# Left-operand loads on another queue, scores between projection products, values behind them, and a pinned order on TensorE and SyncE

## The chip, the core and the metric

The kernel runs on one core of a Trainium2 chip. A core has five engines, each with its own instruction stream: TensorE (PE; its weight loads are listed as PEld), VectorE (DVE), ScalarE (ACT), GpSimd (POOL) and SyncE (SP). SP computes nothing; it only issues transfers (DMAs). ACT and POOL issue transfers too, in line with their own work. What is measured is the time of one execution on the device, in microseconds (us). The median of three runs of the kernel before is 3149.64 us (3143.34 to 3151.75); its profiled execution took 3153.26 us.

## The reference

A transformer block on x of 4 sequences (b), 512 positions, width 1024, all in float32. xn is the layer norm of x. One branch is attention with 32 query heads in 8 groups (g) of 4, one key and one value head per group, head width 128, RMS norm on queries and keys, a linear position bias with a causal mask. The other is a gate: a linear layer with a mixture of low-rank updates, then SiLU.

```
q, k, v = xn @ Wq.T, xn @ Wk.T, xn @ Wv.T          # split into heads
q, k    = rmsnorm(q, q_norm_w), rmsnorm(k, k_norm_w)
scores  = q k^T / sqrt(128) + slope * (pos_k - pos_q), masked above the diagonal
s       = (softmax(scores) @ v) @ Wo.T
base    = xn @ W.T + bias + sum_n (2 * lora_weights[n]) * (xn @ A[n].T) @ B[n].T
out     = x + s * silu(base)
```

## The kernel before

**Three stages.** The first stage normalises and transposes x, keeps the operands of the projections in DRAM (`xs`), and computes the first half of the gate. The second stage, which the change touches, runs over 32 *units*, a unit being a pair (g, b), g outermost, and then computes the second half of the gate for the four sequences (`last_gate`). The third stage multiplies by Wo and combines the branches.

**Projection of a unit.** `project` (L205) computes q, k and v of a unit with Strassen's scheme in one level: for each of two row halves m there are 7 products instead of 8, each of 4 matmuls of 128x128 by 128x384. A unit thus has 14 products, numbered 1 to 14 here. `strassen` (L121) is a generator that stops after each product, so that a caller can put other work between them. Every product takes its own left operand `a`, 256 KB, which `stream` (L396) fetches from `xs` at L399. The pool has 6 buffers for `a`, so the load for a product has to wait until the product six before it is done. Partial sums go through ACT copies (`save`, L215) and DVE additions (`put`, L222 and L224). After 7 products `norm` (L410) takes two of the four row tiles: ACT squares them (L414), DVE sums (L416, L418), POOL takes the inverse root (L420), DVE scales (L421) and transposes in 32x32 blocks into `flat` (L424). After product 14 the other two tiles follow, and then 16 small transfers on SP move the blocks of `flat` into `qkT` (L433); DVE scales the keys into `kT` (L438).

**Scores of a unit.** `attend` (L449) makes 16 score tiles, c = 0 to 15, of 128 rows by 32(c+1) columns (at least 128). For each: a PE matmul into one of 3 PSUM buffers `sc` (L456), on DVE the bias and a row minimum (L465), on ACT the exponential with its row sum into `pr` (L476), which frees the `sc` buffer. Once four tiles are through, DVE takes the reciprocal of the sums (L490), ACT scales the four (L495), and DVE transposes them blockwise into `turned` (L497), of which there is one buffer. When all 16 are done, 16 transfers on SP, of 160 KB each, move `turned` into `pt` (L505), one buffer again.

**Values of a unit.** `values` (L511) makes four tiles `ov` with 1, 2, 3 and 4 matmuls (128x128 by 128x512) from `pt` and v (L516). ACT copies each out (`oh`, L524, two buffers) and issues its store `ot` (L525).

**The loop** (L579 to L590). For a unit, `fill` is the generator of the next unit's projection. The values of the unit before are written with one step of `fill` after each of their four tiles, then the scores with one step after every two tiles, then the rest of `fill`.

**What sets the order.** The program is recorded and then ordered by a planner with its own estimate of durations. It may move an instruction past others of its engine wherever data allow; the text above is only its input. Each engine then executes its own list strictly in that order, and an instruction that waits holds all that stand behind it. Buffers that are still read or written, and data not yet there, become waits on semaphores. Transfers that SP and ACT issue share eight completion counters, dealt out in turn in the planner's order; before a transfer is issued, it waits until the one eight places before it has landed, whichever of the two queues issued that one.

In the order that the planner made of the kernel before, PE has in each unit: products 1 to 4 of the next projection, the ten matmuls of the values of the unit before, score tiles 0 and 1, then products with two score tiles between them up to product 11, then products 12 to 14 (half of product 10 stands before and half behind score tile 11). SP has per unit 16 `pt` transfers, 16 `qkT` transfers, then 14 `a` loads.

Of the kernel before, what the change touches and what calls it, by code (L numbers as in the profile page):

```python
# [37 lines left out]
NP = 7  # L38


def _slopes():
    start = 2 ** (-(2 ** (-(math.log2(H) - 3))))
    return [start * start**i for i in range(H)]
# [3 lines left out]
def kernel(  # L47
# [14 lines left out]
):  # L62
    nc = tc.nc
    slopes = _slopes()

    const = ctx.enter_context(tc.tile_pool(name="const", bufs=1))
    dram = ctx.enter_context(tc.tile_pool(name="dram", bufs=1, space=DRAM))
# [53 lines left out]
    def strassen(psum, snap, name, nk, ncols, lhs, rhs, shape, save, put):  # L121

        def product(acc, i, start):
            left, right = lhs(i), rhs(i)
            for k in range(nk):
                nc.tensor.matmul(  # L128
                    acc,
                    lhsT=left[k],  # L130
                    rhs=right[k],
                    start=start and k == 0,
                    stop=k == nk - 1,
                    skip_group_check=True,
                )

        def bank(n):
            return psum.tile([P, ncols], F32, tag="mm", name=f"{n}_{name}")

        def kept(n):  # L140
            return snap.tile(shape, F32, tag="kept", name=f"{n}_{name}")

        u = bank("u")
        product(u, A11B11, True)
        k1 = kept("k1")
        save(k1, u, 11)
        yield
# [37 lines left out]
    with ExitStack() as front:  # L185
# [70 lines left out]
        with ExitStack() as early:  # L256
# [19 lines left out]
            for n in range(NLORA):  # L276
                nc.scalar.dma_start(
                    out=coef[n * RANK : (n + 1) * RANK, :],
# [18 lines left out]
            def add_lora(half):  # L297
                for kc in range(KC):
                    pl = ps_sc.tile([P, 512], F32, tag="sc", name=f"pl_{half}_{kc}")
                    nc.tensor.matmul(  # L300
                        pl,
                        lhsT=laT[:, kc, :],
                        rhs=lb_sb[:, half * 512 : (half + 1) * 512],
                        start=True,
                        stop=True,
                    )
                    w = wfs[half][:, kc].rearrange("p n h -> p (n h)")
                    nc.vector.tensor_tensor(w, w, pl, ALU.add)
# [49 lines left out]
            for b in range(B):  # L358
# [11 lines left out]
                for n, _ in enumerate(work):  # L370
                    if b + 1 < B and n in (2, 9):
                        m = n // 7
# [8 lines left out]
        with ExitStack() as mid:  # L381
# [14 lines left out]
            def stream(name, b):  # L396
                def left(m, i):
                    a = apool.tile([P, KH, P], F32, tag="a", name=f"a_{name}_{m}_{i}")
                    nc.sync.dma_start(out=a, in_=xs[b][m][:, i])  # L399
                    return a  # L400

                return left


            def project_qkv(u, b, right, held):
                flat = unit.tile([P, NT, 4, G + 1, 32], F32, tag="flat", name=f"flat_{u}", bufs=1)
                v = unit.tile([P, NT, HD], F32, tag="v", name=f"v_{u}", bufs=3)
                held["v"] = v

                def norm(t, c):  # L410
                    nc.gpsimd.tensor_copy(v[:, t, :], c[:, G + 1, :])  # L411
                    qk = c[:, 0 : G + 1, :]
                    sq = work.tile([P, G + 1, HD], F32, tag="sq", name=f"sq_{u}_{t}", bufs=1)
                    nc.scalar.activation(sq, qk, AF.Square)  # L414
                    ss = small.tile([P, G + 1], F32, tag="ss", name=f"ss_{u}_{t}")
                    nc.vector.tensor_reduce(ss, sq, AX.X, ALU.add)  # L416
                    ms = small.tile([P, G + 1], F32, tag="ms", name=f"ms_{u}_{t}")
                    nc.vector.tensor_scalar(ms, ss, 1.0 / HD, RMS_EPS, ALU.mult, ALU.add)  # L418
                    inv = small.tile([P, G + 1], F32, tag="inv", name=f"inv_{u}_{t}")
                    nc.gpsimd.tensor_tensor(inv, ms, neg_half, ALU.pow)  # L420
                    nc.vector.tensor_tensor(  # L421
                        qk, qk, inv.unsqueeze(2).to_broadcast([P, G + 1, HD]), ALU.mult
                    )
                    nc.vector.transpose(  # L424
                        flat[:, t], qk.rearrange("p h (a e) -> p a h e", a=4)
                    )

                yield from project(f"p_{u}", b, G + 2, stream(u, b), right, norm)

                qkT = unit.tile([P, NT, 4, G + 1, 32], F32, tag="qkT", name=f"qkT_{u}", bufs=1)  # L430
                for a in range(4):
                    for r in range(4):
                        nc.sync.dma_start(  # L433
                            out=qkT[32 * a : 32 * a + 32, :, r].rearrange("p t h e -> p t (h e)"),
                            in_=flat[32 * r : 32 * r + 32, :, a].rearrange("p t h e -> p t (h e)"),
                        )
                kT = unit.tile([P, 4 * NT, 32], F32, tag="kT", name=f"kT_{u}", bufs=1)
                nc.vector.tensor_scalar(  # L438
                    kT,
                    qkT.rearrange("p t r h e -> p (t r) h e")[:, :, G, :],  # L440
                    w_sb,
                    None,
                    ALU.mult,
                )
                held.update(qkT=qkT, kT=kT)
                yield


            def attend(u, g, b, held, bias):  # L449
                qkT, kT = held["qkT"], held["kT"].rearrange("p c e -> p (c e)")  # L450

                def scores(i, t, den):
                    c = 4 * i + t
                    w = max(32 * (c + 1), P)
                    sc = ps_sc.tile([P, S], F32, tag="sc", name=f"sc_{u}_{c}")
                    nc.tensor.matmul(  # L456
                        sc[:, :w],
                        lhsT=qkT[:, i, t, 0:G, :].rearrange("p h e -> p (h e)"),
                        rhs=kT[:, :w],
# [22 lines left out]
                for i in range(NT):  # L482
# [8 lines left out]
                    for t in range(NT):  # L491
                        c = 4 * i + t
                        n = max(c + 1, 4)
                        pr = prs[t][:, : 32 * n]
                        nc.scalar.activation(pr, pr, AF.Copy, scale=rden[:, t : t + 1])  # L495
                        c0 = 4 * first_pair[i]
                        nc.vector.transpose(  # L497
                            turned[:, c0 : c0 + n, t, :],
                            pr.rearrange("p (n e) -> p n e", n=n),
                        )  # L500
                pt = unit.tile([P, npairs, G, P], F32, tag="pt", name=f"pt_{u}", bufs=1)
                src = turned.rearrange("p (n m) t e -> p n m (t e)", m=4)
                for h in range(G):
                    for m in range(4):
                        nc.sync.dma_start(  # L505
                            out=pt[32 * m : 32 * m + 32, :, h, :],
                            in_=src[32 * h : 32 * h + 32, :, m, :],
                        )
                held["pt"] = pt

            def values(u, g, b, held):  # L511
                pt, v = held["pt"], held["v"]
                for i in range(NT):
                    ov = ps_ov.tile([P, S], F32, tag="ov", name=f"ov_{u}_{i}")
                    for j in range(i + 1):
                        nc.tensor.matmul(  # L516
                            ov,
                            lhsT=v[:, j, :],
                            rhs=pt[:, first_pair[i] + j].rearrange("p h q -> p (h q)"),
# [12 lines left out]

            def load_qkv(g):
                raw[g] = weight_tile(G + 2, f"w_{g}")
                nc.sync.dma_start(
                    out=raw[g][:, :, 0:G, :],
                    in_=wq[g].rearrange("p k (n h) -> p k n h", n=G),
                )
                nc.sync.dma_start(
                    out=raw[g][:, :, G:, :],  # L540
                    in_=wkv[g].rearrange("p k (n h) -> p k n h", n=2),
                )
# [25 lines left out]
            def bias_of(g):  # L568
# [3 lines left out]
                )  # L572
                return bias

            load_qkv(0)
            for _ in start_project(*units[0]):
                pass
            before = None
            for n, (g, b) in enumerate(units):  # L579
                if b == 0:  # L580
                    bias = bias_of(g)
                fill = start_project(*units[n + 1]) if n + 1 < len(units) else last_gate(0)
                if before is not None:
                    for _ in values(f"{before[0]}_{before[1]}", *before, held.pop(before)):
                        next(fill, None)
                for _ in attend(f"{g}_{b}", g, b, held[g, b], bias):
                    next(fill, None)
                for _ in fill:
                    pass
                before = g, b  # L590
            fill = last_gate(1)
            for _ in values(f"{before[0]}_{before[1]}", *before, held.pop(before)):
                next(fill, None)
            for _ in fill:
                pass
            for b in range(2, B):
                for _ in last_gate(b):
                    pass


    with ExitStack() as back:
        wpool = back.enter_context(tc.tile_pool(name="wo", bufs=4))
        apool = back.enter_context(tc.tile_pool(name="heads", bufs=2))
# [166 lines left out]
```

## Time and profile before

| | us |
|---|---|
| median of the runs shown (lowest, highest) | 3149.64 (3143.34, 3151.75) |
| the profiled execution, and its span | 3153.26, 3151.5 |
| first scores (start of the units' steady run) | at 240.83 |
| start of the values in the first and in the thirtieth unit | at 279.25 and 2125.33 |
| end of the second stage on PE, start of the third | at 2323.0 and 2337.7 |
| PE busy, of the span | 2826.4 (90%) |
| DVE, ACT, POOL busy | 1315.5, 838.2, 562.3 |

The values start 29 times between 279.25 and 2125.33, so that a unit takes 63.66 us on average (1846.08 / 29). In the profile an arrow names what a wait ended on; a transfer is written destination<-source, SPq and ACTq are the issuing queues, and buffer numbers are left out of names, so that `u_p` and `c_p` are PSUM tiles of a projection.

### The profile page before, as it was taken

The numbers are of one execution on the slowest core, as the hardware profiler recorded it, in microseconds if no ns is written. First come the engines' busy times: TensorE is split into PE (matmuls) and PEld (weight loads), VectorE is DVE, ScalarE is ACT, GpSimd is POOL, SyncE is SP. The second block draws the span as 40 slices with busy tenths as digits, with TensorE's granted clock in tenths as the row PEclk, the third lists the DMA queues.
The fourth block names the chain that finished last, engine by engine and source line by source line (L and its number), as shares of the span: only waits on it lengthen the run. The fifth ranks groups of instructions, "written<-read, shape, count | busy, mean of one in ns | idle before, by whom it ended". The sixth has DMA issues, their size and how long they took to land.

```text
span 3151.5 us, 26438 instructions
## 1 busy us (share of the span) xinstructions
PE 2826.4 (90%) x8104; PEld 1551.5 (49%) x8104; DVE 1315.5 (42%) x3003; ACT 838.2 (27%) x2132; POOL 562.3 (18%) x532
## 2 busy tenths in 40 slices
PE   6898998989898989898989888988889999999997
PEld 4765554545454545454545444544654444344443
DVE  4225443454345434444445445443332232323464
ACT  1113433343343333333334333433200000000010
POOL 5430120121020120121012102011030031311311
PEclk9999999999999989999999999998989999999999
DMA  7544465555555556446546555465662333434364
GB/s 270 221 128 133 120 180 146 143 160 137 143 168 143 138 142 185 120 126 187 157 120 168 142 156 152 122 147 145 211 232 108 113 138 122 173 127 140 134 218 148
DMA packets 392220, 485.73 MB, mean 154 GB/s; under 512 B 31760, under 2 KB 269328, under 8 KB 389520
## 3 DMA queue, kind: packets, MB, share of 16 engines
q1 hardware_dynamic: 360032, 391.75, 44.8%
q10 hardware_dynamic: 20272, 50.34, 4.3%
q0 software_dynamic: 11776, 41.95, 3.3%
q8 instruction: 66, 1.08, 0.1%
q14 instruction: 74, 0.61, 0.1%
HBM read 265.82 MB, written 92.27 MB: 114 GB/s over the span
## 4 chain that ended last, share of the span: by engine, by line
PE 52%; SPq 16%; DVE 13%; POOL 7%; DMA 6%; issue 3%; ACT 3%; ACTq 0%; POOLq 0%; DVEq 0%
PE c_o L128 13%; SPq L505 11%; PE u_o L128 10%; PE c_p L128 9%; PE sc L456 6%; PE ov L516 6%; SPq L433 5%; PE u_p L128 5%; DVE turned L497 3%; POOL inv L420 3%; PE c_f L128 2%; DMA qkT<-flat 2%; DVE c_p L421 2%; PE u_f L128 2%; DVE flat L424 2%
## 5 line engine op out<-in xcount | busy, mean ns | idle before, releaser
L516 PE MATMUL ov<-pt,v 128*128 128x512 f32 x640 | 356.3, 722 | 151.7 <-DMA qkT<-flat 116.1
L456 PE MATMUL sc<-kT,qkT 128*128 128x128 f32 (+12 forms) x1024 | 311.8, 424 | 78.8 <-ACT pr L476 63.8
L128 PE MATMUL u_p<-t_q,a 128*128 128x384 f32 x1024 | 377.1, 508 | 2.5 <-DMA a<-xs 2.2
L128 PE MATMUL c_p<-t_q,a 128*128 128x384 f32 x1024 | 352.0, 487 | 2.0 <-DMA a<-xs 1.7
L128 PE MATMUL c_p<-w,a 128*128 128x384 f32 x1024 | 352.9, 487 | 0.0
L476 ACT ACTIVATE pr<-sc,low 128x128 f32<-128x128 f32 (+12 forms) x512 | 251.5, 493 | 341.2 <-DVE low L465 333.1
L516 PEld LDWEIGHTS ov<-pt,v 128*128 128x128 f32 x640 | 147.1, 236 | 353.6 <-issue 329.6
L465 DVE CUSTOM_DVE_ANT_0 sc<-sc,bias 128x128 f32<-128x128 f32 (+12 forms) x512 | 225.6, 459 | 212.9 <-PE sc L456 208.7
L456 PEld LDWEIGHTS sc<-kT,qkT 128*128 128x128 f32 x1024 | 186.2, 199 | 213.9 <-ACT pr L476 91.2
L411 POOL COPY v<-c_p 128x128 f32<-128x128 f32 x128 | 37.1, 294 | 1357.8 <-DVE c_p L222 1218.7
L128 PEld LDWEIGHTS u_p<-t_q,a 128*128 128x128 f32 x1024 | 199.2, 197 | 144.4 <-issue 29.9
L128 PEld LDWEIGHTS c_p<-t_q,a 128*128 128x128 f32 x1024 | 192.1, 190 | 134.5 <-issue 12.0
L128 PEld LDWEIGHTS c_p<-w,a 128*128 128x128 f32 x1024 | 194.2, 191 | 123.8
L128 PE MATMUL u_o<-t_o,s 128*128 128x512 f32 x512 | 236.3, 605 | 17.5 <-DVE k_o L676 17.3
L495 ACT ACTIVATE pr<-pr,rden 128x128 f32<-128x128 f32 (+12 forms) x512 | 236.5, 522 | 15.9 <-DVE rden L490 15.9
L497 DVE STREAM_TRANSPOSE turned<-pr 128x128 f32<-128x128 f32 (+12 forms) x512 | 218.3, 456 | 38.2 <-ACT pr L495 38.2
L684 DVE TENSOR_TENSOR c<-c_o,k_o 128x512 f32<-128x512 f32 x96 | 66.2, 690 | 360.0 <-ACT k_o L674 190.3
L524 ACT COPY oh<-ov 128x512 f32<-128x512 f32 x128 | 75.0, 586 | 514.9 <-PE ov L516 486.5
L438 DVE TENSOR_SCALAR kT<-qkT,w_sb 128x512 f32<-128x512 f32 x32 | 15.6, 486 | 466.9 <-DMA qkT<-flat 418.1
L674 ACT COPY k_o<-u_o 128x512 f32<-128x512 f32 x48 | 28.1, 586 | 660.2 <-PE u_o L128 660.2
L420 POOL TENSOR_TENSOR inv<-ms,neg_half 128x5 f32<-128x5 f32 x128 | 149.5, 1168 | 253.1 <-DVE ms L418 199.5
L128 PE MATMUL u_p<-w,a 128*128 128x384 f32 x512 | 175.6, 486 | 0.0
(111 smaller groups left out, 3125.6 us busy)
## 6 DMA issues: line engine op xcount, KB each, us to landing
a<-xs SPq DMA_DIRECT2D x448, 256.0 KB, 3.0
pt<-turned SPq DMA_DIRECT2D x512, 160.0 KB, 3.8
qkT<-flat SPq DMA_DIRECT2D x512, 80.0 KB, 2.4
ot<-oh ACTq DMA_DIRECT2D x128, 256.0 KB, 2.9
o<-ot SPq DMA_DIRECT2D x64, 512.0 KB, 3.2
sums<-c POOLq DMA_DIRECT2D x48, 512.0 KB, 4.7
old<-sums SPq DMA_DIRECT2D x48, 512.0 KB, 4.0
w<-in_wq_dram SPq DMA_DIRECT2D x8, 2048.0 KB, 9.5
```

The costliest lines, as they stand in the source:

```text
L128: nc.tensor.matmul(acc, lhsT=left[k], rhs=right[k], start=start and k == 0, stop=k == nk - 1, skip_group_check=True,)
L420: nc.gpsimd.tensor_tensor(inv, ms, neg_half, ALU.pow)
L433: nc.sync.dma_start(out=qkT[32 * a : 32 * a + 32, :, r].rearrange("p t h e -> p t (h e)"), in_=flat[32 * r : 32 * r + 32, :, a].rearrange( ...
L456: nc.tensor.matmul(sc[:, :w], lhsT=qkT[:, i, t, 0:G, :].rearrange("p h e -> p (h e)"), rhs=kT[:, :w], start=True, stop=True,)
L465: nc.vector.tensor_tensor_reduce(out=sc[:, :w], in0=sc[:, :w], in1=bias[:, at : at + w], scale=-1.0, scalar=3.0e38, op0=ALU.add, op1=ALU.m ...
L476: nc.scalar.activation(pr[:, :w], sc[:, :w], AF.Exp, bias=low, scale=-1.0, accum_out=den[:, t : t + 1],)
L495: nc.scalar.activation(pr, pr, AF.Copy, scale=rden[:, t : t + 1])
L497: nc.vector.transpose(turned[:, c0 : c0 + n, t, :], pr.rearrange("p (n e) -> p n e", n=n),)
L505: nc.sync.dma_start(out=pt[32 * m : 32 * m + 32, :, h, :], in_=src[32 * h : 32 * h + 32, :, m, :],)
L516: nc.tensor.matmul(ov, lhsT=v[:, j, :], rhs=pt[:, first_pair[i] + j].rearrange("p h q -> p (h q)"), start=j == 0, stop=j == i,)
L524: nc.scalar.copy(oh, ov.rearrange("p (h q) -> p h q", h=G))
L684: nc.vector.tensor_tensor(dst, acc, kept, ALU.add)
```

## The change

Four edits, all in the second stage.

1. The loads of `a` are issued by ACT instead of SP.
2. The step `spread` (the 16 transfers from `turned` to `pt`) becomes a function of its own, called at the end of a unit's turn.
3. The loop first takes 6 products of the next projection (`LEAD`), then the scores with one product after every two tiles, then the rest of the projection (which ends with `qkT` and `kT` of the next unit), then all values of the unit before without products between them, then `spread` for this unit. The second gate's first part fills the last unit as before; its second part no longer has the last values between its products.
4. While `in_order` is set, matmuls on PE and transfers on SP other than the loads of `a` keep the order of the text. ACT, DVE and POOL are still ordered by the planner.

```diff
+LEAD = 6
+    in_order = [False]
+    def sync_dma(**kw):
+        ins = nc.sync.dma_start(**kw)
+        if in_order[0]:
+            tc.keep_in_program_order(ins)
+    def matmul(*args, **kw):
+        ins = nc.tensor.matmul(*args, **kw)
+        if in_order[0]:
+            tc.keep_in_program_order(ins)
...
             def stream(name, b):
...
-                    nc.sync.dma_start(out=a, in_=xs[b][m][:, i])
+                    nc.scalar.dma_start(out=a, in_=xs[b][m][:, i])
...
+            def spread(u, held):
                 pt = unit.tile([P, npairs, G, P], F32, tag="pt", name=f"pt_{u}", bufs=1)
...
-                        nc.sync.dma_start(
+                        sync_dma(
                             out=pt[32 * m : 32 * m + 32, :, h, :],
...
+            in_order[0] = True
             load_qkv(0)
...
                 fill = start_project(*units[n + 1]) if n + 1 < len(units) else last_gate(0)
-                if before is not None:
-                    for _ in values(f"{before[0]}_{before[1]}", *before, held.pop(before)):
-                        next(fill, None)
+                for _ in range(LEAD):
+                    next(fill, None)
                 for _ in attend(f"{g}_{b}", g, b, held[g, b], bias):
                     next(fill, None)
                 for _ in fill:
                     pass
+                if before is not None:
+                    for _ in values(f"{before[0]}_{before[1]}", *before, held.pop(before)):
+                        pass
                 before = g, b
-            fill = last_gate(1)
+                spread(f"{g}_{b}", held[before])
+            for _ in last_gate(1):
+                pass
             for _ in values(f"{before[0]}_{before[1]}", *before, held.pop(before)):
-                next(fill, None)
-            for _ in fill:
                 pass
...
+    in_order[0] = False
```

The matmuls of `strassen`, `attend` and `values`, and the transfers of `qkT`, `pt` and the weights (`load_qkv`), go through the two new helpers; `load_gate` does not.

In the changed program, as the planner ordered it, PE has in each unit: the ten value matmuls, products 1 to 6, score tiles 0 and 1, and from there a product after every two tiles, ending with tiles 14 and 15 and product 14. SP has 16 `qkT` transfers and then 16 `pt` transfers. The 14 loads of `a` stand among ACT's own instructions.

More of the change, by code (lines that the diff above doesn't have):

```diff
@@ L127, in product @@
             for k in range(nk):
-                nc.tensor.matmul(
+                matmul(
                     acc,
@@ L299, in add_lora @@
                     pl = ps_sc.tile([P, 512], F32, tag="sc", name=f"pl_{half}_{kc}")
-                    nc.tensor.matmul(
+                    matmul(
                         pl,
@@ L455, in scores @@
                     sc = ps_sc.tile([P, S], F32, tag="sc", name=f"sc_{u}_{c}")
-                    nc.tensor.matmul(
+                    matmul(
                         sc[:, :w],
@@ L504, in attend @@
                     for m in range(4):
-                        nc.sync.dma_start(
+                        sync_dma(
                             out=pt[32 * m : 32 * m + 32, :, h, :],
@@ L515, in values @@
                     for j in range(i + 1):
-                        nc.tensor.matmul(
+                        matmul(
                             ov,
@@ L534, in load_qkv @@
                 raw[g] = weight_tile(G + 2, f"w_{g}")
-                nc.sync.dma_start(
+                sync_dma(
                     out=raw[g][:, :, 0:G, :],
@@ L538, in load_qkv @@
                 )
-                nc.sync.dma_start(
+                sync_dma(
                     out=raw[g][:, :, G:, :],
```

## The prediction

> **What bounds the kernel now.** I read the page first (PE 90% busy, so only PE's idle and slow time can be won), then PE's instructions in order of time over one unit, SP's over the same stretch, the chain of waits, the granted clock in short stretches, and the waits of SP.
>
> ```profile
> PE 2826.4 (90%) x8104; PEld 1551.5 (49%) x8104; DVE 1315.5 (42%) x3003; ACT 838.2 (27%) x2132; POOL 562.3 (18%) x532
> L516 PE MATMUL ov<-pt,v 128*128 128x512 f32 x640 | 356.3, 722 | 151.7 <-DMA qkT<-flat 116.1
> ```
> ```profile
> 1045.92 10.24 PE L516 MATMUL ov<-pt,v 128*128 128x512 f32 x20 [4.52 <-DMA qkT<-flat]
> 1057.17 0.71 PE L456 MATMUL sc<-kT,qkT 128*128 128x128 f32 x4 [1.01 <-DVE kT L438]
> 1057.72 2.75 PE L128 MATMUL u_p<-t_q,a 128*128 128x384 f32 x8
> ...
> 1077.68 0.91 PE L456 MATMUL sc<-kT,qkT 128*128 128x384 f32 x2 [2.15 <-ACT pr L476]
> ```
> ```profile
> 1028.74 14.02 SPq L505 DMA_DIRECT2D pt<-turned  x16
> 1042.85 11.61 SPq L433 DMA_DIRECT2D qkT<-flat  x16
> ```
> ```profile
> 1053.85 2.55 DMA qkT<-flat
> ...
> 1056.63 0.50 DVE kT L438
> ```
> ```profile
> 1045.00:1047.00 2.00, 1.08 (x2) 0.59 (x3) 0.00 (x0) 0.00 (x0) 0.00 (x0) 0.59 0.66 147
> 1047.00:1049.00 2.00, 2.00 (x4) 0.85 (x3) 0.00 (x0) 0.59 (x1) 0.00 (x0) 0.56 0.45 97
> 1049.00:1051.00 2.00, 2.00 (x6) 0.92 (x5) 0.00 (x0) 0.59 (x1) 0.00 (x0) 1.00 0.82 244
> ```
> ```profile
> SPq L399 <- DMA ot<-oh: 149.8, 59, 4.7
> ```
>
> The reader is to see: PE waits 4.52 us for the values' operand, since `pt` leaves SP only after the last `turned`; then 1.01 for the keys, whose 16 transfers stand behind `pt` on SP; then 2.15 for ACT and DVE. After the wait of 4.52 the clock (third column from the end) is 0.59 and 0.56, and the first four value matmuls start 0.86 apart, later ones 0.43. The last line: loads of `a` waited 59 times for a store that has no data in common with them; that is the shared completion counter.
>
> **A unit's floor.** From start to start: 14 products of 2.58 us (36.1), scores 7.86 (0.55, 0.42, 0.59, 0.82, 1.02, 0.59, 0.75, 1.45, 1.67 from the same rows), values 20 x 0.43 = 8.6. Together 52.56, against 63.66 measured. The 11.1 lost: about 4.5 before the values, 2.15 at tile 10, some 0.7 at other waits, some 3.2 of half clock (the values take 10.2 to 11.8), 0.5 that I can't place; I leave that 0.5 in.
>
> **The change, part by part.** I lay out one unit in the new order with the durations of the rows; T = 0 is the end of product 14.
>
> *Keys ahead of `pt` on SP; values and six products as cover.* After sc 15, exp, scaling and transposes run as at 1023.35 to 1028.71, which here ends at T+3. Then the norm of two tiles (L416 0.82, L418 0.17, L420 1.18, L421 0.82, L424 0.83, in the chain 1004.46 to 1013.73): `flat` is done at T+10.5. Sixteen issues take 10.5 to 11.6, landing 2.55: T+24 to 25. PE has ov 8.6 plus 0.7 (the third value tile needs ACT's first copy, which stands behind the scalings and a square) and six products, 15.5: T+24.8. So the 4.52 wait goes, with it the half clock. But on DVE `kT` now stands behind the addition for product 6: 0.52 (L222) + 0.49 + hops, scores at T+26. **Wait 1.2.**
>
> *Loads of `a` on ACT.* An issue there takes 0.33 (the row of `ot`), 14 a unit, 4.6 us; ACT is busy 23 of 62, so by itself nothing. But each load waits for the product six before, and ACT's exponentials stand behind it. Tiles 0 to 9 in ACT's order: the load for product 13 waits for product 7; squares, exponentials, four scalings, then the load for product 14 at T+34.1; next products 1's load after product 9; copy L215 and next product 2's load after product 10. On DVE the bias of tile 4 stands behind POOL's inverse root, done only at T+36. sc 7 needs tile 4's exponential, **0.75** late; sc 9 needs tile 6's, behind copy and load, **0.95** late. Product 10 ends at T+39.6 (26 + four products 10.3 + tiles 0 to 7 2.4 + 0.75, rounded).
>
> *`pt` leaves behind the keys.* Its 16 issues begin at T+21 to 22.5, at 0.88 each (14.02/16): unhindered they end near T+36 and land by T+40. DVE's first `turned` of the next tiles waits for all of them (one buffer) and is reached at T+40.7. That would be free. But the program's counters tie `pt` 12 to the load for product 14, `pt` 13 to next product 1's, `pt` 16 to next product 2's. That last one: product 10 ends 39.6, copy 0.47, issue 0.33, landing 2.7 (median of L399 in this stretch): 43.2. Then `pt` 16, 0.6 and 2.7 landing (the least of L505, the queue being empty): **T+46.4**. DVE stands 5.7 us. Behind it: four `turned` (0.31 each), reciprocal, four scalings (0.43 each), bias 9, exponential 9 at T+50.1. PE, at 48.0 after product 12, needs that buffer for sc 12: **2.2**. sc 13 **0.55**, after tile 10's exponential. sc 15 needs tile 12's exponential, behind three scalings, copy 0.47, an addition and a transpose: **1.35**. Product 14 ends at T+60.3, and ACT and DVE stand as at T = 0.
>
> *Half clock after the 2.2.* Nothing in the trace shows a wait of this length at this place. The nearest row, the 2.15 at tile 10, was followed by 0.91 for the pair in 20 of 30 units and by 1.05 to 1.65 in 10; a full slow stretch costs 4 x 0.43 = 1.7. Between 0 and 1.7 I take a third, **0.5**.
>
> *Others.* The operand sums of a new group on POOL (4 x 3.45) start after product 11, end about T+62, before the first inverse root asks at T+64: nothing; if not covered, up to 3 us in 7 units. Weights (3 MB) go out on SP between `pt` and the next keys, some 20 us of room. The pinned order costs nothing but what is listed.
>
> *Sum.* 52.56 + 0.5 + (0.7 + 1.2 + 0.75 + 0.95 + 2.2 + 0.55 + 1.35) + 0.5 = 61.3 a unit, 2.4 less than 63.66; in 29 units 70. First units: unit 0 has 15.5 of cover where the chain needs 23.3, idle 7.8 against 5.64 before; unit 1 has no values as cover, another 8.5 idle and 1.7 slow, on a turn 9.3 shorter. Last: the two waits of 8.13 and 8.79 before the last values go, while the last scores have short gate products (1.72) as cover and wait 5. Placed one after another (first scores 242.8, unit 2 from 334, 29 x 61.3, then 53 to the end of the last scores' turn and 90 of values and gate) the second stage ends at 2255 instead of 2323, 68 less. Against the profiled execution's 3153.3: 3085; that one stood 3.6 above the median, so **3080**.
>
> [...] After the 2.15 us waits above, 10 of 30 units ran slow. [...] SP's row L399 <- `ot` shows that the two queues are tied. [...] With no tie counted the sum would be that of the first rival.
>
> **Rivals.**
> 1. *The tie doesn't bind* (the loads land earlier, or DVE has slack). Then 2.2, 0.55, 1.35 and the 0.5 fall away: 56.7 a unit, 4.6 x 30 = 138 less, 2940. For it: `pt` itself is done by T+40. Against: the waits stand in the program in every unit.
> 2. *Slower: the tie binds harder.* Place: DVE's first `turned`. The row L399 goes up to 5.4 to landing, L505 to 4.2: 2.7 + 1.5 more, and the wait at sc 12 is then 6.4, past the 4.5 that is always followed by half clock, 1.2 more: 66.7, 3.0 x 29 = 88 slower, 3235 at the most. It decides from 2.4 us more on. For it: two landings in a row, and `pt` keeps the DMA engines 0.85 busy (175 GB/s). Against: by T+39 only two `pt` are under way.
> 3. *Nothing changes*: what leaves the values comes back at the scores, within 9 us of now.
>
> **How the numbers follow.** Forecast 0.57 (its own range 3035 to 3125, 1.5 us a unit either way), rival 1 0.15, rival 2 0.21, rival 3 0.07. Two in ten left out, one below and one above: 2940 to 3185, the middle of rival 2. This kernel's runs tell 0.3%, 9 us, from no change. Faster 0.72, same 0.06, slower 0.22.
>
> **What would show it.** PE before ov: no wait, first matmuls 0.43 apart. SP: `qkT` ahead of `pt`, and `pt` with gaps before the 12th, 13th and 16th. DVE waiting 4 to 7 us in L497 on a `pt` transfer; PE waiting about 2 us at the 416-column tile. A unit of 60 to 62.5 us. I am wrong if ACT's loads hold exponentials for longer than the product they wait for, if `kT` arrives after T+27, or if L497 doesn't wait.

## The result and the profile after

The changed kernel takes 3223.97 us (median of four runs, 3223.44 to 3237.00) against 3150.69 for the kernel before (3143.34 to 3153.59): the ratio is 1.0246, with an interval of 1.0215 to 1.0277. It is slower by 2.5%; 3080 had been forecast, with a range that ended at 3185. The profiled execution took 3237.0 us, with a span of 3235.0.

In the changed kernel every matmul stands under one line, L76, every pinned transfer of SP under L71, and the loads of `a` under L413. First the totals by engine and three groups of PE (busy us, mean ns of one, then idle time ahead of them and what ended it):

```profile
PE 2827.7 (87%) x8104; PEld 1554.7 (48%) x8104; DVE 1312.5 (41%) x3003; ACT 831.4 (26%) x2132; POOL 567.6 (18%) x532
L76 PE MATMUL sc<-kT,qkT 128*128 128x128 f32 (+12 forms) x1024 | 329.4, 436 | 297.4 <-ACT pr L490 235.8
L76 PE MATMUL c_p<-t_q,a 128*128 128x384 f32 x1024 | 410.0, 551 | 0.0
L76 PE MATMUL ov<-pt,v 128*128 128x512 f32 x640 | 290.3, 601 | 15.2 <-ACT oh L539 7.8
```

The scores and the same products in the kernel before, in the same columns:

```profile
L456 PE MATMUL sc<-kT,qkT 128*128 128x128 f32 (+12 forms) x1024 | 311.8, 424 | 78.8 <-ACT pr L476 63.8
L128 PE MATMUL c_p<-t_q,a 128*128 128x384 f32 x1024 | 352.0, 487 | 2.0 <-DMA a<-xs 1.7
```

The values, which waited 151.7 us before, now wait 15.2, and one of their matmuls takes 601 ns instead of 722. But the scores wait 297.4 instead of 78.8, and 235.8 of that is for ACT's exponentials. The products `c_p<-t_q,a`, which follow some of these waits, have become slower as well: 410.0 us instead of 352.0, for the same matmuls.

PE over one unit, in order of time (start, us, then in brackets the idle time ahead and its releaser):

```profile
995.74 2.74 PE L76 MATMUL ov<-pt,v 128*128 128x512 f32 x6
998.73 6.28 PE L76 MATMUL ov<-pt,v 128*128 128x512 f32 x14 [0.25 <-ACT oh L539]
...
1021.53 0.71 PE L76 MATMUL sc<-kT,qkT 128*128 128x128 f32 x4 [1.04 <-DVE kT L452]
...
1031.82 0.70 PE L76 MATMUL sc<-kT,qkT 128*128 128x256 f32 x2 [0.41 <-ACT pr L490]
...
1042.62 1.43 PE L76 MATMUL sc<-kT,qkT 128*128 128x320 f32 x2 [7.04 <-ACT pr L490]
1043.85 4.83 PE L76 MATMUL c_p<-t_q,a 128*128 128x384 f32 x8
...
1052.33 1.61 PE L76 MATMUL sc<-kT,qkT 128*128 128x416 f32 x4
...
1056.36 1.83 PE L76 MATMUL sc<-kT,qkT 128*128 128x480 f32 x4
```

One wait decides: 7.04 us at tile 9 (128x320). The product behind it takes 4.83 us instead of 2.74, and tile 9 itself 1.43. Tiles 12 to 15 (128x416 to 128x512) don't wait at all. The clock tells why the product is slow (columns: stretch, length, busy time of PE, PEld, DVE, ACT and POOL, then the granted clock, DMA share, GB/s):

```profile
1037.00:1039.00 2.00, 0.00 (x0) 0.00 (x0) 0.00 (x0) 0.00 (x0) 0.00 (x0) 0.70 0.69 224
...
1043.00:1045.00 2.00, 2.00 (x4) 1.13 (x4) 1.32 (x6) 1.93 (x7) 0.00 (x0) 0.50 1.05 407
...
1047.00:1049.00 2.00, 2.00 (x6) 1.25 (x5) 0.00 (x0) 0.00 (x0) 0.00 (x0) 0.74 1.06 355
```

In the first row no engine computes at all. The chain of waits across that gap (start, us, what), and the sum of one kind of ACT's waits (us in total, times, longest):

```profile
1032.52 2.60 PE u_p L76 x8
...
1035.19 3.55 DMA a<-xs
...
1038.76 2.79 DMA pt<-turned
...
1041.62 0.71 DVE turned L511 x3
...
1042.38 0.20 ACT pr L490
...
1042.62 1.43 PE sc L76 x2
```
```profile
ACT pr L490 <- DVE turned L511: 200.9, 31, 7.5
```

Product 10 ends, the load for next product 2 is issued and lands 3.55 us later; only then SP issues `pt` 16, which takes 2.79; then DVE may write `turned` for tile 0; then ACT may write an exponential, and PE gets its `sc` buffer. The last line, with 31 such waits, names the link that the prediction didn't have: an *exponential* waits for a *transpose*. `pr` has six buffers, so tile 6's exponential is written where tile 0's lay, and that one is free only when DVE has transposed tile 0.

### The profile page after: what moved, and what is told of

The parts are those of the page before. It is cut to its first block, busy times and chain, and to the rows that moved or that the text cites. A ratio compares the mean times of both kernels' runs of the same rounds, so it can differ in the third digit from the quotient of the medians.

```text
span 3235.0 us, 26441 instructions
## 1 busy us (share of the span) xinstructions
PE 2827.7 (87%) x8104; PEld 1554.7 (48%) x8104; DVE 1312.5 (41%) x3003; ACT 831.4 (26%) x2132; POOL 567.6 (18%) x532
## 4 chain that ended last, share of the span: by engine, by line
PE 69%; DMA 12%; DVE 7%; issue 3%; ACT 3%; SPq 2%; POOL 2%; ACTq 0%; DVEq 0%; POOLq 0%
PE c_p L76 16%; PE c_o L76 13%; PE u_p L76 12%; PE u_o L76 10%; PE sc L76 9%; DMA a<-xs 5%; PE ov L76 5%; DMA pt<-turned 3%; PE c_f L76 3%; SPq L71 2%; DVE turned L511 2%; PE u_f L76 2%; DMA qkT<-flat 1%; DMA row<-in_x_dram 1%; ACT pr L490 1%
## 5 line engine op out<-in xcount | busy, mean ns | idle before, releaser
L76 PE MATMUL sc<-kT,qkT 128*128 128x128 f32 (+12 forms) x1024 | 329.4, 436 | 297.4 <-ACT pr L490 235.8
L76 PE MATMUL c_p<-t_q,a 128*128 128x384 f32 x1024 | 410.0, 551 | 0.0
L76 PEld LDWEIGHTS sc<-kT,qkT 128*128 128x128 f32 x1024 | 182.3, 200 | 432.1 <-ACT pr L490 261.0
L76 PE MATMUL c_p<-w,a 128*128 128x384 f32 x1024 | 362.3, 498 | 0.0
L76 PE MATMUL u_p<-t_q,a 128*128 128x384 f32 x1024 | 352.1, 487 | 0.0
L76 PEld LDWEIGHTS c_p<-t_q,a 128*128 128x128 f32 x1024 | 227.6, 222 | 172.1 <-issue 69.8
L76 PE MATMUL ov<-pt,v 128*128 128x512 f32 x640 | 290.3, 601 | 15.2 <-ACT oh L539 7.8
L238 DVE TENSOR_TENSOR c_p<-c_p,k_p 128x384 f32<-128x384 f32 x192 | 103.6, 539 | 442.0 <-ACT k_p L229 239.2
L76 PEld LDWEIGHTS c_p<-w,a 128*128 128x128 f32 x1024 | 196.8, 196 | 130.9 <-issue 23.8
L76 PEld LDWEIGHTS u_p<-t_q,a 128*128 128x128 f32 x1024 | 195.1, 191 | 129.7 <-issue 0.9
L76 PE MATMUL u_o<-t_o,s 128*128 128x512 f32 x512 | 237.1, 607 | 18.7 <-DVE k_o L695 18.4
L76 PEld LDWEIGHTS ov<-pt,v 128*128 128x128 f32 x640 | 119.8, 191 | 173.5 <-issue 131.9
L229 ACT COPY k_p<-u_p 128x384 f32<-128x384 f32 x192 | 90.6, 472 | 403.3 <-PE u_p L76 300.2
L76 PE MATMUL u_p<-w,a 128*128 128x384 f32 x512 | 175.7, 486 | 0.0
```

Source lines behind the costliest of these rows:

```text
L76: ins = nc.tensor.matmul(*args, **kw)
L229: nc.scalar.copy(kept, acc.rearrange("p (n h) -> p n h", n=nh))
L238: nc.vector.tensor_tensor(dst, acc, kept, ALU.add)
```

## The experiments

All are edits of the changed kernel unless it says otherwise. "Tie" is the wait of a transfer on SP for one of ACT's, through the shared counters. What the traces of the two kernels show of these: the 1865 transfers of SP and ACT signal their landing on the same eight semaphores (233 or 234 on each), the 96 of POOL on eight others (12 on each), and no transfer was issued before the one ahead of it on its semaphore had landed. In the unit shown above `pt` 12, 13 and 16 stand on their semaphores behind loads of `a` that landed at 1032.70, 1033.93 and 1038.74, and the issue of each ended 0.60 us later. In all, the pinned transfers of SP waited 151 times for a load of `a`, 422.1 us.

**1. A pool of their own for the small exponentials.** If the six buffers carry the wait, it goes when tiles 0 to 3 don't share them.

```diff
-                    pr = work.tile([P, S], F32, tag="pr", name=f"pr_{u}_{c}", bufs=6)
+                    if i == 0:
+                        pr = work.tile([P, P], F32, tag="pr0", name=f"pr_{u}_{c}", bufs=4)
+                    else:
+                        pr = work.tile([P, S], F32, tag="pr", name=f"pr_{u}_{c}", bufs=6)
```

> The exponentials of tiles 0 to 3 get four small buffers of their own, so that tile 6 no longer has to wait until tile 0 has been transposed into turned. Everything else is the changed kernel. Theory A (what I hold now): the 16th pt transfer waits, by the shared completion counter, for a load of a on ACT that waits for product 10; the first transpose into turned waits for it; tile 6's exponential waits for that transpose because there are only six buffers; score tile 9 waits for it, 7.0 us and then half clock. With the small buffers the wait at tile 9 falls to about 1 and some 2 us come back at the 416-column tile, as in my prediction's layout: 61 to 62 us a unit instead of 64.9, 3224 - 29 x 3.4 = 3125 (3090 to 3150). The transfers pt 12 to 16 leave as late as now. Theory C (loads on ACT hold the exponentials up, whatever the buffers): tile 9 still waits over 5 us, time within 20 of 3224.

Measured: 3050.96 us, 0.9664 of before (0.9646 to 0.9682), 39 below the range that theory A gave. The wait at tile 9 is gone in every unit, although `pt` leaves SP no faster. One longer wait is left, at tile 13 and not, as expected, at tile 12:

```profile
1007.64 24.41 SPq L71 DMA_DIRECT2D pt<-turned  x16
```
```profile
1036.73 1.02 PE L76 MATMUL sc<-kT,qkT 128*128 128x448 f32 x2 [2.73 <-ACT pr L493]
```

So 173 us of the changed kernel hang on which buffer tile 6 is written to.

**2. The loads on POOL's queue.** This takes the tie away and leaves the buffers.

```diff
-                    nc.scalar.dma_start(out=a, in_=xs[b][m][:, i])
+                    nc.gpsimd.dma_start(out=a, in_=xs[b][m][:, i])
```

> The 14 loads of a per unit are issued by GpSimd, whose transfers have completion counters of their own; PE, SP and their orders stay as in the changed kernel. Theory A: pt transfers no longer wait for loads, the 16th leaves at about T+36 to 38 instead of 43 (T: end of product 14), the first transpose into turned hardly waits, tile 9 waits at most 2, no half clock: 57 to 58 us a unit, 3224 - 29 x 7 = 3020 (2970 to 3070). Theory B (the tie doesn't matter; the 16 DMA engines are simply full when loads come from a second queue in between, so pt takes 22 us): the same bytes go on a third queue, pt takes as long, 3224 within 30. Theory C: ACT is free of loads, so faster too, but pt would still spread over 22 us.

Measured: 3111.84 us, 0.9863 (0.9841 to 0.9886).

```profile
1034.79 15.31 SPq L71 DMA_DIRECT2D pt<-turned  x16
```
```profile
pt<-turned SPq DMA_DIRECT2D x512, 160.0 KB, 6.4
```

The issues of `pt` close up from 21.93 us to 15.31, as they should without a tie. But the median from issue to landing (last figure) grows from 4.3 to 6.4 us, and tile 9 still waits 1.4 to 6.0. The chain of waits leads back to such a landing:

```profile
1048.64 9.41 DMA pt<-turned
...
1058.13 0.71 DVE turned L511 x3
...
1058.89 0.20 ACT pr L490
...
1059.13 1.43 PE sc L76 x2
```

Of the 200 us expected from a `pt` without its tie 112 came. So in this unit the later landings hold the first `turned`; how much of the missing 88 us is theirs was not measured.

**3. A seventh buffer for the left operand.**

```diff
-            apool = mid.enter_context(tc.tile_pool(name="left", bufs=6))
+            apool = mid.enter_context(tc.tile_pool(name="left", bufs=7))
```

> Seven buffers for the left operands instead of six, otherwise the changed kernel. Each load may go one product earlier. Theory A: with seven buffers the 16th pt transfer is tied to the load of next product 3, which waits for product 10, the same product as now; so nothing changes: 3224 within 10, tile 9 waits 7 us. Theory B or a plain lack of buffers: loads are earlier and out of the way of pt, faster by 30 or more.

Measured: 3228.65 us, 1.0235 (1.0219 to 1.025); tile 9 waits as in the changed kernel (7.21 in the unit at 1041.88). With seven buffers each load waits for the product seven before, but `pt` 16 is now tied to the load one product later: it is again product 10 that sets it free.

**4. The loads back on SP, all else as changed.**

```diff
-                    nc.scalar.dma_start(out=a, in_=xs[b][m][:, i])
+                    nc.sync.dma_start(out=a, in_=xs[b][m][:, i])
```

> Undoes one part: the loads of a go back to SP, the rest of the change stays. Theory A: all transfers of a unit stand in one list again, in which the load for product 7 is behind 16 qkT and 16 pt transfers. These leave by T+36 unhindered (no tie across queues), so turned and tile 9 hardly wait, but product 7 waits from T+27 to T+39: 12 us and half clock: 68 to 70 us a unit, 3224 + 29 x 4 = 3340 (3290 to 3400). Theory C: ACT free of loads, faster than 3224.

Measured: 3584.01 us (one run). The direction was right, the expected time 244 short:

```profile
L76 PE MATMUL c_p<-w,a 128*128 128x384 f32 x1024 | 422.1, 563 | 435.3 <-DMA a<-xs 435.3
```

A product waits 12 to 23 us for its load in most units, since the load stands in SP's list behind transfers of `qkT` and `pt` that wait for DVE. So the move to ACT's queue is no cost of the change but what makes its order bearable.

**5. Small pool and loads on POOL together.** Is the wait left at tile 13 in experiment 1 the tie?

> The changed kernel with both edits together: the 128-column exponentials in a pool of their own (four buffers), and the loads of a on POOL's queue. Theory A (what is left in the small-tile version, the wait of 2.7 us at the 448-column tile, is the tie of pt to loads that wait for a product): pt leaves SP in about 15 us instead of 24.4, that wait goes, the unit falls from 58.2 to about 55.5, time 2960 to 2990. Theory B (with the tie gone the transfers only queue on the DMA engines: landing of pt 6.5 us instead of 4): the first turned still comes no earlier than T+43, the late wait stays between 1.5 and 4 us, time 3030 to 3080, no better than the small-tile version by more than 20 us.

Measured: 3053.88 us, 0.968 (0.9639 to 0.9721), the same as experiment 1. Its time is theory B's, but the reason isn't. Here are SP, DVE, ACT and PE around tile 13, one after another:

```profile
1020.64 14.22 SPq L71 DMA_DIRECT2D pt<-turned  x16
```
```profile
1047.43 0.59 DVE L479 CUSTOM_DVE_ANT_0 sc<-sc,bias 128x416 f32<-128x416 f32 x1
...
1047.94 1.99 DVE L514 STREAM_TRANSPOSE turned<-pr 128x128 f32<-128x128 f32 x8
```
```profile
1049.14 0.56 ACT L493 ACTIVATE pr<-sc,low 128x352 f32<-128x352 f32 x1 [2.22 <-DVE turned L514]
```
```profile
1049.84 1.86 PE L76 MATMUL sc<-kT,qkT 128*128 128x448 f32 x2 [2.74 <-ACT pr L493]
```

`pt` has left SP by 1034.86, and even with 9.7 us to landing, the longest of this unit's sixteen, it is there by 1044.6, before the first transpose. DVE transposes tiles 0 to 7 only at 1047.94, because in its list they stand behind the bias of tile 12 (128x416). Tile 10's exponential (128x352) needs tile 4's buffer, so it waits for these transposes, and tile 13 needs tile 10's `sc` buffer. That is a closed turn of PE, DVE and ACT in which no transfer has a part: the 2.73 of experiment 1 and the 2.74 here are the same wait.

**6. The small pool in the kernel before.** The edit of experiment 1, made there.

> The kernel before with one edit: the 128-column exponentials in a pool of their own. Theory A (the six buffers cost time only in the new order, since in the order before no turned of tile 0 stands behind a late pt when tile 6 is written; its wait of 2.15 us at tile 10 is put down to DVE's work on the bias): the wait at tile 10 stays at 2.0 to 2.3, the 4.5 before the values too, time within 15 us of the kernel before. Rival (the six buffers held the kernel before as well, at tile 10): that wait goes, 2.15 x 30 = 65 us less, time near 3085, and the gain of the small-tile version belongs to the buffers rather than to the order.

Measured: 3153.35 us, 0.9996 (0.9982 to 1.0009). The six buffers cost nothing in the order before; theory A.

**7. Seven products ahead of the scores**, with the small pool.

```diff
-LEAD = 6
+LEAD = 7
```

> The small-tile version with seven products instead of six ahead of the first scores. Theory A (pt 16 is tied to the load after product 10, so its landing is counted from a product, and scores put one product, 2.58 us, later need it that much later): the wait at the 448-column tile falls from 2.7 to under 0.7, and the 1.04 at the keys goes too since kT is there by then; unit about 55 to 56 us, time 2955 to 2990. Rival (the end of the unit, scores then exponentials, scaling, transposes and the next keys, is the chain that turns): what is won at these two waits comes back at the last scores or before the next first scores, time 3035 to 3060.

Measured: 3009.85 us, 0.9537 (0.9504 to 0.957), between the two theories. The 1.04 at the keys went; the wait at tile 13 only fell from 2.73 to 2.46, and some came back elsewhere, as the rival feared, though at other places: the third value tile waits 1.4 to 1.6 in 23 units (0.3 in experiment 1) and tile 5 about 0.6. My theory counted that wait from `pt` 16 and was wrong; in its trace too DVE's transposes stand behind the bias of tile 12, so the closed turn of experiment 5 moves along with the scores.

**8. The loads on ACT's queue alone, in the kernel before.** Only the diff's one line in `stream`; PE and SP are ordered by the planner, the loop is the old one.

> The kernel before with one part of the change alone: the loads of a on ACT's queue, order left to the planner. Theory A (the loads tie both queues through the shared counters, whatever the order): with values first, pt waits on loads behind products and the values wait longer than 4.5 us, unit over 66 us, time 3200 or more. Rival (the loads on ACT are harmless or help SP, and what cost time in the changed kernel was only its own order): SP has 14 issues a unit less, qkT and pt leave earlier, time 3100 to 3150.

Measured: 2975.44 us (one run), better than either theory allowed, so it was repeated:

> The kernel before with the loads of a on ACT's queue and nothing else, timed in rounds, since its one time of 2975 stood against both theories. Theory A (the loads alone carry a gain that the rest of the change gives back): 2965 to 2990, unit 57.7 to 59.1 from values to values. Rival (that time was one odd execution): above 3050.

Measured: 2977.71 us, 0.9443 (0.9412 to 0.9474).

```profile
L516 PE MATMUL ov<-pt,v 128*128 128x512 f32 x640 | 296.9, 621 | 59.8 <-DMA qkT<-flat 36.5 <-DMA pt<-turned 18.3 <-issue 4.9
...
L456 PE MATMUL sc<-kT,qkT 128*128 128x128 f32 (+12 forms) x1024 | 293.6, 414 | 41.6 <-ACT pr L476 37.4 <-DVE kT L438 4.2
```

The one line alone takes 92 us of waiting off the values, 59 us of their slow running and 37 off the waits of the scores: 188, against 175 measured. The planner answers that line with another order (it draws the scores together behind the values), so line and answer gain together, and the share of each stays open. The tie is there too: in this kernel `pt` leaves SP over some 20 us.

**9. The same with the small pool.**

> The kernel before with the loads of a on ACT's queue and the 128-column exponentials in a pool of their own. Theory A (the 1.0 to 1.3 us that PE waits at the 128-column scores comes from three score tiles in PSUM and ACT, not from the six buffers): within 12 us of the same kernel with six buffers for all, 2963 to 2990. Rival (the buffers hold it here as in the changed kernel): that wait goes, about 30 us less, 2940 to 2955.

Measured: 2973.54 us, 0.9435 (0.9409 to 0.946): no difference, theory A.

**10. Three sizes of exponentials.** If the closed turn of experiment 5 is real, giving tile 10 another buffer must move the wait, not end it.

```diff
-                    pr = work.tile([P, S], F32, tag="pr", name=f"pr_{u}_{c}", bufs=6)
+                    if i < 2:
+                        pr = work.tile([P, P * (i + 1)], F32, tag=f"pr{i}", name=f"pr_{u}_{c}", bufs=4)
+                    else:
+                        pr = work.tile([P, S], F32, tag="pr", name=f"pr_{u}_{c}", bufs=4)
```

> The changed kernel with three pools of exponentials: four of 128 columns, four of 256, four of 512. Theory C (what is left in the small-tile version is a closed turn that pt has no part in: the exponential that needs a used buffer waits for DVE's transposes, and these stand behind a bias of a late score tile): with tile 10 no longer on tile 4's buffer the wait leaves the 448-column tile, and since tile 12 now needs tile 8's buffer and DVE has the transposes behind the bias of tile 14, it comes back at the 512-column tile: bias 0.67, transposes of nine tiles 2.4, exponential 0.6, so 3.0 to 4.0 us; time 3050 to 3100. Rival (late pt is what is left): no wait of over 1 us at either tile, time 2970 to 3010.

Measured: 3118.25 us, 0.9886 (0.9866 to 0.9906). DVE, ACT and PE:

```profile
1008.65 0.67 DVE L479 CUSTOM_DVE_ANT_0 sc<-sc,bias 128x480 f32<-128x480 f32 x1 [0.25 <-PE sc L76]
...
1009.23 3.63 DVE L514 STREAM_TRANSPOSE turned<-pr 128x128 f32<-128x128 f32 x12
```
```profile
1011.68 0.61 ACT L493 ACTIVATE pr<-sc,low 128x416 f32<-128x416 f32 x1 [6.52 <-DVE turned L514]
```
```profile
1012.43 2.07 PE L76 MATMUL sc<-kT,qkT 128*128 128x512 f32 x2 [3.82 <-ACT pr L493]
```

The wait left tile 13 and came back at tile 15, behind the bias of tile 14, within the 3.0 to 4.0 expected. All 30 steady units also run slow after it, which the expectation had not priced; hence 18 us above its range.

**11. The order left free.** The written loop and the loads stay as changed, but nothing is pinned.

```diff
-            in_order[0] = True
+            in_order[0] = False
```

> The changed kernel with the order of PE and SP left to the planner (loads on ACT and the spread written as in the changed kernel). In its order the first nine score tiles stand among products 4 to 6 of the turn and tiles 9 to 15 after six or seven more products, between the values. Theory A (the pinned place of tile 9, ahead of product 11, is what costs the 7 us and the half clock): with products in front of tile 9 that wait is covered; no wait of over 3 us in a unit, time 2970 to 3030. Rival (pt tied to the loads is late in any order): tile 9 or the values wait 4 us or more, time 3100 to 3200.

Measured: 2969.09 us, 0.9414 (0.9393 to 0.9436), 255 us under the changed kernel. Between tiles 8 and 9 now stand almost ten products and the first value tile; tile 9 still waits in most units, mostly 1 to 1.4 us, but in five of them 4.7 to 4.8, where theory A had none over 3:

```profile
1022.11 1.02 PE L76 MATMUL ov<-pt,v 128*128 128x512 f32 x2
1027.88 3.89 PE L76 MATMUL sc<-kT,qkT 128*128 128x320 f32 x6 [4.75 <-ACT pr L490]
```

**12 and 13. One order pinned at a time.** The helper of the other engine loses its `keep_in_program_order`.

> The changed kernel with TensorE alone in program order, SyncE's left to the planner. Theory D (TensorE's order is what costs: tile 9 stands ahead of product 11 and has nothing in front of it): the wait of 7 us at tile 9 and the half clock behind it stay, 3190 to 3250. Rival (SyncE's order costs, by sending pt behind all keys): 2960 to 3030.

Measured: 3239.13 us, 1.0264 (1.0229 to 1.0299).

> The changed kernel with SyncE alone in program order, TensorE's left to the planner, which puts tiles 9 to 15 among the values. Theory D: within 20 us of the kernel with both left free, 2955 to 2990. Rival (SyncE's order costs): 3190 to 3250.

Measured: 2985.72 us, 0.9455 (0.9431 to 0.9479). Pinned alone, SyncE's order costs 17 us and TensorE's 270; both together cost 255:

```profile
1043.10 1.44 PE L74 MATMUL sc<-kT,qkT 128*128 128x320 f32 x2 [7.01 <-ACT pr L488]
```

That line is from the run with TensorE alone pinned. The wait at tile 9 is back at its full length.

**14. Free order and small pool**, the edits of 1 and 11.

> The changed kernel, both orders left free, and the 128-column exponentials in a pool of their own. In its order tiles 0 to 12 stand among products 3 to 5 and tiles 13 to 15 between the second and third value tile. Theory D with the six buffers (with both orders free, tile 9 still waits 1.4 to 4.8 us in some units, 85 us in all on ACT's exponentials, since it needs tile 0's buffer): half of it or more goes, 2905 to 2945. Rival (the wait only moves to the 448-column tile, as it did in the pinned order): 2955 to 2980.

Measured: 2850.57 us, 0.9029 (0.9006 to 0.9052), the fastest of all, and 54 us under the lower end of what was expected. PE and SP:

```profile
985.78 1.88 PE L76 MATMUL ov<-pt,v 128*128 128x512 f32 x4
987.50 2.58 PE L76 MATMUL sc<-kT,qkT 128*128 128x448 f32 x6
```
```profile
1004.05 27.32 SPq L71 DMA_DIRECT2D pt<-turned  x16
```

`pt` takes 27 us to leave SP, tied as ever, and PE hardly waits for it: thirteen tiles are done before the first transpose is needed, the last three stand among the values. A unit takes 55.2 us, 2.6 above the floor that the prediction worked out.

The runs by loads, order and buffers (medians in us; 3584 is one run):

| loads of `a` | order of PE and SP | six `pr` buffers | small tiles apart |
|---|---|---|---|
| SP | planner, loop of before | 3151 (before) | 3153 |
| ACT | planner, loop of before | 2978 | 2974 |
| ACT | planner, changed loop | 2969 | 2851 |
| ACT | PE and SP pinned | 3224 (changed) | 3051 |
| POOL | PE and SP pinned | 3112 | 3054 |
| SP | PE and SP pinned | 3584 | |

## Why the prediction was wrong

**What held.** The wait ahead of the values is gone and their clock is full, as said (1.00 granted from 995.74 to 1005.01 in the unit shown); the third value tile waits 0.25 (0.7 predicted), the keys 1.04 (1.2), tile 7 0.41 (0.75). The tie is as it was laid out: `pt` 16 behind next product 2's load, that behind product 10. With T = 0 at the end of product 14 (995.9 in the unit shown), the first `turned` starts at T+45.7, after DVE has waited 5.48; 46.4 and 5.7 were predicted.

**The step that failed** is the place where PE pays for that late `turned`. "Sc 9 needs tile 6's, behind copy and load, 0.95 late", the prediction says, and lets the wait for `pt` fall on tile 12, at 2.2. It followed tile 6's exponential through ACT's queue (squares, copies, loads) and did not ask where the exponential is written. With six `pr` buffers that is tile 0's, so the first `turned` is needed six tiles after tile 0, not at the end of DVE's slack. PE is ready for tile 9 at T+39.7 (1035.58 in the unit shown), and by the prediction's own count for tile 12 only at T+48.0: the same late transpose meets 8 us less of cover. Tile 9 waited 6.7 to 8.0, and the waits of 2.2, 0.55 and 1.35 at tiles 12, 13 and 15, which came to 4.1, did not occur, since everything behind tile 9 was already late. Experiment 1 shows it: other buffers for tiles 0 to 3, the tie unchanged, and the wait is gone.

**The term that was mis-sized** is the half clock: 0.5 a unit, taken as a third of 1.7 because a wait of 2.2 is followed by slow running only at times. After 7 us it followed every time: the `c_p<-t_q,a` group lost 58 us, 1.9 a unit, and tile 9 some 0.7 more. So waits and half clock together came to about 11.4 a unit (0.25, 1.04, 0.41, 7.1 and 2.6 of slow running) where 8.2 was predicted.

**The sum.** From the values of the first unit to those of the thirtieth (344.73 to 2238.60) there are 29 turns of 65.3 us, against 61.3: 116 of the 152 us by which the profiled execution, 3237.0 against 3085, missed. Some 13 of the 116 lie in four turns of 68 us, whose keys waited 2.4 to 3.4 instead of 1.04. The first turns end 10.7 late (344.73 against 334), as the wait at tile 9 is in them too (5.90 in the second). The rest, some 25, came at the end: waits of 7.25 at the last keys and 8.02 at the last tile 9, and 7.35 before the last values, one of the two waits that were to go.

**"The pinned order costs nothing but what is listed"** was wrong as well, by the same omission: left free, the planner puts products in front of tile 9; in the pinned order PE stands still. Experiments 12 and 13 put 270 us on TensorE's order and 17 on SyncE's. And where the prediction costs the loads on ACT "by itself nothing", SP's row of waits, which it shows, could have said something: on SP the loads waited 59 times for a store. Moved alone, with the order that the planner then makes, they bring 175 (experiment 8); that it is this wait which they escape was not shown.

**Rival 2** came nearest: slower through the tie, at most 3235, and 3224 was measured. Its place, DVE's first `turned`, was right. Its cause, longer landings, was not: 3.55 and 2.79 us gave a first `turned` no later than predicted. What made the tie bind harder was the buffer, which took away the cover, and not the transfer, so that its number came close by luck.

## What to carry to other kernels

When a step is made later, list who reads its result *and* who writes into the buffers that it frees: count the buffers of every pool on the way, and ask at which tile the pool comes round, for that is where the wait falls. A pinned order should be tried with each engine's order set free before it is kept; here it turned a gain of 5.9% into a loss of 2.5%. And a pool may be split by the size that tiles really have: 2 KB per partition for four small tiles were worth 119 us in one order, 173 in another, and nothing in a third, so the worth of a buffer is a property of the order.

## What was not expected of the hardware

**The clock after short waits.** Equal waits are followed by slow running in some units and not in others. At 2.74 us (experiment 5) it was 14 units of 30, at 3.82 (experiment 10) and 7 (changed kernel) all of them, at 2.46 (experiment 7) 8 of 30, from the fourth on exactly every fourth:

```profile
1144.01 1.02 PE L76 MATMUL sc<-kT,qkT 128*128 128x448 f32 x2 [2.46 <-ACT pr L493]
1144.87 2.74 PE L76 MATMUL c_p<-w,a 128*128 128x384 f32 x8
...
1200.36 1.86 PE L76 MATMUL sc<-kT,qkT 128*128 128x448 f32 x2 [2.46 <-ACT pr L493]
1202.01 3.51 PE L76 MATMUL c_p<-w,a 128*128 128x384 f32 x8
```

The same wait, the same work, and only the second runs slow. So the wait's length alone doesn't decide. Neither does its place among the four units of a group: in experiment 5 the slow units fall on every place of the four. What separates them is in the traces' record of the granted clock. In every trace of this case the stretches at half clock begin on one grid with a step of 3.41 us. These are steps of experiment 7's grid, the first two holding most of the two waits of 2.46 (columns as before, the granted clock third from the end):

```profile
1142.10:1145.52 3.42, 1.51 (x5) 0.87 (x6) 2.18 (x11) 2.21 (x8) 0.00 (x0) 1.00 0.20 66
...
1196.72:1200.13 3.41, 1.18 (x4) 0.37 (x2) 2.75 (x11) 0.47 (x2) 0.29 (x1) 1.00 1.04 404
1200.13:1203.54 3.41, 3.18 (x5) 1.76 (x6) 2.12 (x7) 3.23 (x11) 0.00 (x0) 0.50 1.07 373
```

PE is idle for 1.9 us of the first, and full clock goes on (1.00 in the next step too); it is idle for 2.2 us of the second, and the third is at half clock. The seventeen traces agree. In the stretch from the first scores to the last, 437 steps at full clock were followed by half clock, and in 418 of these PE was idle for 2.0 us or more; 8359 were followed by full clock, and in four of these it was idle as long, at most 2.02. In the traces of the two kernels alone it is 88 steps, all with 2.01 us of idle or more, against 930 with 2.01 or less. After a step at half clock full clock came back only when PE had been idle for 0.58 us or less of it. So in these runs a wait between 2.0 and 4.0 us cost half clock or not by where it fell on the grid; one of 4.0 or more, by an estimate from the 2.0 and the 3.41, always leaves 2.0 in some step, and the waits ahead of the values in the kernel before, 4.06 to 4.93 us, were followed by half clock (0.50) in all 30 units. A wait of 2.46 or 2.74 us can't fill a step: 2.0 us of the 3.41 were enough.

**One transfer, three queues.** The same 14 loads a unit, in the same pinned order of PE, gave 3584 us from SP, 3224 from ACT and 3112 from POOL. What differed was not the time that an issue takes (0.32, 0.33 and 0.54 us) but what each load stood behind: SP's waiting `qkT` and `pt`, the counters shared with SP, or, from POOL, neither of the two.
